# Hybrid block, attention stage: the next image's normalisation gets its rate through a PSUM bank and VectorE, nine key tiles later

## The chip, the cores and the metric

The kernel runs on one core of one Trainium2 chip. The metric is the device time of one execution in microseconds (us); less is better. The core has a matrix engine (PE), a vector engine (DVE), an activation engine (ACT), a general-purpose engine (POOL) and a queue engine (SP) that issues the DMAs. Each engine executes its own instructions in the order in which they were issued to it, and waits on semaphores for the others. PE writes to PSUM banks; ACT and DVE read and write both PSUM and SBUF; POOL here works on SBUF only.

## The reference

Input `x` is 4 images of 128 channels x 64 x 64. Layer 0 is a state-space convolution block. Layer 1 takes each image as 4096 tokens of 128 channels; its first half is the additive attention that this case is about:

```python
def _L1_attn_ref(x, Wt, Wx, bh, Wa, ba):            # x: (4, 4096, 128), 32 hidden units
    q = jnp.einsum('bld,ud->blu', x, Wt)
    k = jnp.einsum('bld,ud->blu', x, Wx)
    beta = jnp.tanh(q[:, :, None, :] + k[:, None, :, :] + bh)
    alpha = jnp.tanh(jnp.einsum('bsju,u->bsj', beta, Wa[:, 0]) + ba[0])
    alpha = jax.nn.softmax(alpha, axis=-1)
    return jnp.einsum('bsj,bjd->bsd', alpha, x)

x = x + _L0_conv_ref(_gn(x), ...)                    # layer 0
t = _to_tokens(x)
t = t + _L1_attn_ref(_ln_t(t), ...)                  # _ln_t: (v - m) / sqrt(var + 1e-5) over channels
t = t + _L1_ffn_ref(_ln_t(t), ...)                   # a recurrence over the tokens
```

## The kernel before

Three stages run one after the other: layer 0 up to about 4045 us of the span, the attention (`_rational`) to about 11340 us, and the recurrence (`_chunked`) after it. Only the attention is touched.

`_rational` writes the sum over the 32 units of tanh as a few quotients of products. Keys and queries become products of exponentials (`F` for the keys of an image, `E` and `cE` for a block of 512 queries), and a matmul over groups of 64 or 32 rows gives a denominator (`pd` bank) or a numerator (`pn` bank) for 128 keys x 512 queries.

The order of the work is written out by hand. The outer loop is over 4 images `b`, the next one over 8 blocks `s` of 512 queries (so 32 blocks in all, counted 0 to 31 here), and the inner one over 32 key tiles `jt` of 128 keys. In each key tile there are three units, A, B1 and B2, with two banks each:

- PE: `lower` makes the unit's denominators into `pd` (2 buffers of two banks), `upper` its numerators into `pn` (3 single banks); both are line L1212.
- ACT: `inverse` takes Ln of a denominator (L1231) and Exp of the negative (L1232), 1024 columns each, into an `ra` (3 buffers) or an `rb` (4 buffers) tile in SBUF.
- DVE: `times` multiplies each half with its `pn` bank (L1227).
- POOL: adds the units, `ra + rb` for B1 at L1349 and for B2 of the tile before at L1334.
- DVE: adds the two halves of the tile before into its slice of `A` (L1346). Slice `A[:, jt, :]` holds the scores of key tile `jt`.

At the end of a block ACT takes tanh and exp of all of `A` (L1384, L1385), and PE multiplies with the transposed image `xT` into the single bank named `ct` (L1360, pool `psW`, one buffer, function `pw`). The last twelve of these products, key tiles 20 to 31, are done in key tiles 2 to 13 of the next block (the dictionary `middle`).

Small steps are put between the key tiles by the dictionary `between`: what is entered at `jt` is issued at the end of that tile's work. The tuples at the head of the file say at which tile:

- `CLOSE_AT = (14, 16, 17, 18, 19, 20, 22)`: the closing of the block before: the copy from `ct`, the softmax denominator, four reciprocals (DVE, L1258), and `end` (PE L1262, DVE product L1263, POOL add `xr + rec` L1264 and the store).
- `NORM_AT = (15, 17, 19, 20)`: the four steps of `norm_steps` for 512 columns of the next image. They occur in all blocks of images 0 to 2, so in 24 blocks.
- `QUERIES_AT = (24, 26)`: the two query exponentials of the next block, which use the `ct` bank: PE L1134, ACT L1135, and a maximum on DVE (L1137).

In the first block of an image, `turn` (four PE transposes and a DVE copy) is also put in at tiles 22 to 29, and in block 0 at 16 to 23.

The four steps of `norm_steps` are `centre` (PE mean into a `pn` bank, DVE subtraction in place), `square` (ACT Square into an `rb` buffer named `sq`), `rate` (PE mean of the squares into a `pn` bank; ACT Ln at L71 and Exp of -0.5 times it at L72, in `_rsqrt`), and `scale` (POOL product in place, L1164). The normalised image is used by the next image's first queries, keys and transposes, all after the block in which the step is done, except that the last block of an image reads columns 0 to 511, normalised seven blocks before.

Of the kernel before, what the change touches and what calls it, by code (L numbers as in the profile page):

```python
# [9 lines left out]
AF = mybir.ActivationFunctionType  # L10
ALU = mybir.AluOpType
# [15 lines left out]
JT = L // P  # L27
# [13 lines left out]
PARTS = ((0, 4), (4, 12), (12, 20), (20, 32))  # L41
LAST_PARTS = ((0, 8), (8, 16), (16, 24), (24, 29), (29, 32))
CLOSE_AT = (14, 16, 17, 18, 19, 20, 22)
NORM_AT = (15, 17, 19, 20)
QUERIES_AT = (24, 26)
NOW = 20
REACH = 21.0
# [5 lines left out]
def _mm(nc, out, lhsT, rhs, n, start=True, stop=True):  # L53

    for c in range(0, n, MM):
        nc.tensor.matmul(out[:, c : c + MM], lhsT, rhs[:, c : c + MM], start=start, stop=stop)  # L56
# [12 lines left out]
def _rsqrt(nc, out, var, eps):  # L69

    nc.scalar.activation(out, var, AF.Ln, bias=eps)  # L71
    nc.scalar.activation(out, out, AF.Exp, scale=-0.5)  # L72
# [73 lines left out]
@with_exitstack  # L146
def _bounded(
    ctx: ExitStack,
    tc: tile.TileContext,
    flag,  # L150
    x1,
    x, in_wT, conv_w, conv_b, sa_w, sa_b, xpT, xpR, dtwT, dtb, A_quads, Ds,
    on_g, on_b, n1_g, n1_b, out_wT, WtT, WxT, Wt, Wx, bh, Wa, ba, W, WT, VT, gamma, beta,
    out,
):
    nc = tc.nc
    const = ctx.enter_context(tc.tile_pool(name="fconst", bufs=1))
    dram = ctx.enter_context(tc.tile_pool(name="gdram", bufs=1, space=DRAM))
    k = _Consts(tc, const)
    x2 = dram.tile([B, P, L], F32, name="x2")  # L160

    with tc.manual_schedule():
        _layer0(tc, k, x, x1, in_wT, conv_w, conv_b, sa_w, sa_b, xpT, xpR, dtwT, dtb, A_quads, Ds,
                on_g, on_b, n1_g, n1_b, out_wT)
    top = const.tile([P, TOPS], F32, name="top")
    with tc.manual_schedule():
        _rational(tc, k, x1, x2, top, Wt, Wx, bh, Wa, ba)
    with tc.manual_schedule():
        _chunked(tc, k, flag, top, x2, W, WT, VT, gamma, beta, out)
# [876 lines left out]
def _rational(ctx, tc, k, x1, x2, top, Wt, Wx, bh, Wa, ba):  # L1046
# [8 lines left out]
    nc = tc.nc  # L1055
# [14 lines left out]
    def pd():  # L1070
        return psD.tile([P, 2, QB], F32, name="pd", tag="pd")

    def pn():
        return psN.tile([P, QB], F32, name="pn", tag="pn")

    def pw():
        return psW.tile([P, QB], F32, name="ct", tag="ct")
# [23 lines left out]
    ps = pd()  # L1101
# [6 lines left out]
    ps = pd()  # L1108
# [20 lines left out]
    blocks = [slice(c * QB, (c + 1) * QB) for c in range(nq)]  # L1129
    tops = iter(range(TOPS))  # L1130

    def exponent(ps, w, src, i, out, bias=0.0):

        nc.tensor.matmul(ps, w[:, i * P : (i + 1) * P], src, start=True, stop=True)  # L1134
        nc.scalar.activation(out, ps, AF.Exp, bias=bias)  # L1135
        n = next(tops)
        nc.vector.tensor_reduce(top[:, n : n + 1], ps, AX.X, ALU.max)  # L1137


    def norm_load(b, xn, cols):  # L1140
        nc.sync.dma_start(xn[:, cols], x1[b, :, cols])

    def norm_steps(xn, cols, alloc):

        xc = xn[:, cols]
        n = cols.stop - cols.start
        held = {}

        def centre():
            ps = alloc()  # L1150
            _mm(nc, ps, k.avg, xc, n)
            nc.vector.tensor_tensor(xc, xc, ps, ALU.subtract)

        def square():
            held["sq"] = rb.tile([P, CH], F32, name="sq", tag="rb")[:, 0:n]
            nc.scalar.activation(held["sq"], xc, AF.Square)

        def rate():
            ps = alloc()
            _mm(nc, ps, k.avg, held["sq"], n)  # L1160
            _rsqrt(nc, held["sq"], ps, k.eps5)

        def scale():
            nc.gpsimd.tensor_tensor(xc, xc, held["sq"], ALU.mult)  # L1164

        return centre, square, rate, scale

    def keys(F, xn, c, ps, i):

        exponent(ps, w_k, xn[:, blocks[c]], i, F[:, i, blocks[c]], b_k[:, i : i + 1])  # L1170
# [100 lines left out]
    xn = two.tile([P, L], F32, name="xn")  # L1271
# [13 lines left out]
    A = big.tile([P, JT, QB], F32, name="A")  # L1285
    E = two.tile([P, 2, QB], F32, name="E")
    for i in range(2):
        keys(F, xn, 0, pn(), i)
# [3 lines left out]
    start = 0  # L1292
# [3 lines left out]
    for c in range(1, nq):  # L1296
        for i in range(2):
            between.setdefault(2 * c - 2 + i, []).append(lambda c=c, i=i, xn=xn: keys(F, xn, c, pw(), i))
    for c in range(nq):
        between.setdefault(16 + c, []).append(lambda c=c, xn=xn: turn(xT, xn, c))  # L1300
    for b in range(B):
        upcoming = None
        for s in range(nq):
# [4 lines left out]
            if b + 1 < B:  # L1308

                if s == 0:  # L1310
                    upcoming = two.tile([P, L], F32, name="xn")
                norm_load(b + 1, upcoming, blocks[s])
                for at, go in zip(NORM_AT, norm_steps(upcoming, blocks[s], pn)):
                    between.setdefault(at, []).append(go)
            if more:
                E_next = two.tile([P, 2, QB], F32, name="E")
# [47 lines left out]
            held = {}  # L1364
# [33 lines left out]
            if more:  # L1398
                nc.vector.tensor_tensor(A[:, 0, :], held["A"][:, 0, :], held["A"][:, 1, :], ALU.add)
                first = held["first"]  # L1400
                start = 1
# [11 lines left out]
            if turned:  # L1413
                xn = upcoming
# [250 lines left out]
```

## Time and profile before

| what | value |
|---|---|
| median of 3 runs (lowest to highest) | 11600.68 us (11594.8 to 11604.92) |
| the profiled execution: its time, its span | 11599.52 us, 11597.8 us |
| mean granted TensorE clock | 0.935 |
| attention stage, 4045 to 11340 us: PE, ACT, DVE, POOL busy | 7057, 7024, 5513, 5194 us of 7295 |
| L1164 POOL `xn<-xn,sq`, 128x512 | 24 of 1.27 us (and 4 of 128x1024 before the first block) |
| L1156 Square, L71 Ln, L72 Exp on ACT, 128x512 | 24 each, 0.61, 0.67 and 0.63 us |
| L1264 POOL `xr<-xr,rec`, 128x512 | 32 of 1.27 us |

The span runs from the first to the last instruction of the profiled execution; its time is that of the same execution, and the median comes from three executions. Where a line of the profile has a bracket, it says how long the engine was idle before the instruction and who released it. A group of instructions has its count after an x. PEclk is the granted share of TensorE's clock.

### The profile page before, as it was taken

How to read it: one execution, taken by the hardware profiler on the slowest of the kernel's cores; microseconds unless marked ns; L12 is line 12 of the kernel's file. 1: busy time of each engine (PE TensorE's matmuls, PEld its weight loads, DVE VectorE, ACT ScalarE, POOL GpSimd, SP SyncE). 2: the span in 40 equal slices, each digit the busy share in tenths (PEclk: the TensorE clock that was granted, in tenths of full speed). 3: DMA queues.
4: the chain of work that ended last, by engine and by line, in shares of the span. 5: the costliest groups of instructions: out<-in, count | busy, mean ns of one | idle time of the engine just before them, and what ended most of it. 6: DMA issues, size and time to landing. Idle time of an engine off the chain costs nothing.

```text
span 11597.8 us, 111820 instructions
## 1 busy us (share of the span) xinstructions
PE 10265.4 (89%) x36210; PEld 3139.3 (27%) x36210; DVE 8992.9 (78%) x10066; ACT 9467.7 (82%) x10209; POOL 8626.5 (74%) x3703
## 2 busy tenths in 40 slices
PE   6787787778777699999999999999999999999997
PEld 2121121122111132232233223323323233333334
DVE  4998899889889677777777777777777777777773
ACT  3556656656555599999999999999999999999995
POOL 3999889889889677767766776767677767776773
PEclk8898898888888799999999999999999999999998
DMA  4888778778778300000000000000000000000001
GB/s 118 189 182 195 169 179 192 178 173 190 180 169 194 85 1 3 6 3 4 6 3 3 3 6 3 3 3 6 3 3 3 6 2 3 3 4 3 2 3 60
DMA packets 225333, 737.77 MB, mean 64 GB/s; under 512 B 41105, under 2 KB 41937, under 8 KB 223713
## 3 DMA queue, kind: packets, MB, share of 16 engines
q1 hardware_dynamic: 221760, 729.96, 26.7%
q8 instruction: 286, 4.69, 0.2%
q14 instruction: 311, 2.54, 0.1%
q10 hardware_dynamic: 2976, 0.58, 0.0%
HBM read 612.95 MB, written 117.44 MB: 63 GB/s over the span
## 4 chain that ended last, share of the span: by engine, by line
PE 50%; ACT 10%; DVE 3%; issue 3%; POOL 0%; DMA 0%; POOLq 0%; DVEq 0%; SPq 0%; ACTq 0%
PE pn L1212 26%; PE pd L1212 16%; PE ct L1360 4%; ACT A L1384 4%; ACT A L1385 2%; DVE rb L1227 2%; ACT rb L1231 1%; ACT rb L1232 1%; PE ct L1134 1%; ACT ra L1231 1%; PE vy L1559 1%; DVE A L1346 0%; PE ct L1262 0%; PE pn L56 0%; ACT L1384 0%
## 5 line engine op out<-in xcount | busy, mean ns | idle before, releaser
L1212 PE MATMUL pn<-cE,F 32*128 32x512 f32 (+1 forms) x12288 | 4691.2, 651 | 189.9 <-DVE rb L1227 86.0
L1212 PE MATMUL pd<-E,F 32*128 32x512 f32 (+1 forms) x12288 | 3481.5, 649 | 20.4 <-DVE ra L1239 15.5
L1349 POOL TENSOR_TENSOR ra<-ra,rb 128x1024 f32<-128x1024 f32 x993 | 2637.0, 2656 | 1077.5 <-DVE rb L1227 1077.3
L1227 DVE TENSOR_TENSOR rb<-rb,pn 128x512 f32<-128x512 f32 x3972 | 2566.0, 681 | 960.0 <-ACT rb L1232 369.5
L626 POOL TENSOR_TENSOR dBu<-dtdu,bbcc 128x1024 f32<-128x1024 f32 x1024 | 2397.9, 2367 | 217.8 <-DMA dtdu<-ddd 158.8
L1334 POOL TENSOR_TENSOR ra<-ra,rb 128x1024 f32<-128x1024 f32 x993 | 2345.6, 2362 | 228.4 <-DVE rb L1227 123.9
L1232 ACT ACTIVATE rb<-rb 128x1024 f32<-128x1024 f32 x1986 | 2099.5, 1057 | 62.9
L1231 ACT ACTIVATE rb<-pd 128x1024 f32<-128x1024 f32 x1986 | 2004.6, 1009 | 112.5 <-PE pn L1212 84.9
L1212 PEld LDWEIGHTS pn<-cE,F 32*128 32x128 f32 (+1 forms) x12288 | 1367.1, 186 | 2553.9 <-DVE rb L1227 1386.2
L668 PE MATMUL py<-h,gather 128*32 128x512 f32 x4096 | 1300.7, 701 | 471.3 <-POOL h L651 359.7
L1227 DVE TENSOR_TENSOR ra<-ra,pn 128x512 f32<-128x512 f32 x1986 | 1288.2, 683 | 528.1 <-PE pn L1212 325.0
L1212 PEld LDWEIGHTS pd<-E,F 32*128 32x128 f32 (+1 forms) x12288 | 933.2, 186 | 1646.9 <-issue 820.7
L621 ACT ACTIVATE pa<-dtdu,a_neg 128x1024 f32<-128x1024 f32 x1024 | 1145.2, 1118 | 53.1 <-DVE h L641 32.1
L651 POOL TENSOR_TENSOR h<-h,bbcc 128x1024 f32<-128x1024 f32 x384 | 911.7, 2374 | 346.0 <-ACT carry L649 336.5
L641 DVE TENSOR_TENSOR_SCAN pa<-pa,carry,dBu 128x1024 f32<-128x1024 f32 x480 | 1124.5, 2343 | 23.1 <-ACT pa L621 11.3
L1232 ACT ACTIVATE ra<-ra 128x1024 f32<-128x1024 f32 x993 | 1049.7, 1057 | 31.4
L1360 PE MATMUL ct<-A,xT 128*128 128x512 f32 x2048 | 1052.3, 642 | 8.8 <-ACT A L1385 8.8
L1231 ACT ACTIVATE ra<-pd 128x1024 f32<-128x1024 f32 x993 | 1001.3, 1008 | 31.7 <-PE pd L1212 26.4
L649 ACT COPY carry<-pa 128x1 f32<-128x1 f32 x640 | 102.5, 160 | 1044.2 <-DVE h L648 1042.2
L1346 DVE TENSOR_TENSOR A<-ra 128x512 f32<-128x512 f32 x993 | 743.3, 749 | 115.9 <-POOL ra L1334 115.8
L648 DVE TENSOR_TENSOR h<-pa,bbcc 128x1024 f32<-128x1024 f32 x640 | 783.8, 1225 | 59.0 <-PE py L668 0.9
L641 DVE TENSOR_TENSOR_SCAN h<-pa,carry,dBu 128x1024 f32<-128x1024 f32 x288 | 675.0, 2344 | 171.0 <-PE py L668 141.1
(291 smaller groups left out, 8740.9 us busy)
## 6 DMA issues: line engine op xcount, KB each, us to landing
bbcc<-bcd SPq DMA_DIRECT2D x1024, 256.0 KB, 6.9
dtdu<-ddd SPq DMA_DIRECT2D x1024, 256.0 KB, 7.2
ddd<-dd SPq DMA_DIRECT2D x64, 1024.0 KB, 5.1
src<-src SPq DMA_DIRECT2D x64, 512.0 KB, 8.3
xs<-in_x_dram SPq DMA_DIRECT2D x16, 512.0 KB, 7.5
src<-xs SPq DMA_DIRECT2D x16, 512.0 KB, 3.0
bcd<-bc SPq DMA_DIRECT2D x64, 128.0 KB, 2.0
src<-xsT SPq DMA_DIRECT2D x16, 512.0 KB, 5.4
```

The lines of the kernel that those rows point to most:

```text
L621: nc.scalar.activation(dA, its[m].DT[r][:, 0, :], AF.Exp, scale=a)
L626: nc.gpsimd.tensor_tensor(dBu, its[m].DT[r][:, 1, :], its[m].BC[q][:, 0, :], ALU.mult)
L641: nc.vector.tensor_tensor_scan(to[:, step], dA[:, step], live.pop(("dBu", u))[:, step], 0.0 if m % nch == 0 else its[m - 1].carry[:, col : ...
L651: nc.gpsimd.tensor_tensor(h, h, cc, ALU.mult)
L668: nc.tensor.matmul(it.y[to, c], gather, live["h", v][:, c], start=False, stop=(q == QS - 1))
L1212: nc.tensor.matmul(ps[a], F[lo:hi, i, jt * P : (jt + 1) * P], side[lo:hi, i, :], start=True, stop=True)
L1227: nc.vector.tensor_tensor(r[:, a, :], r[:, a, :], ns[a], ALU.mult)
L1231: nc.scalar.activation(r, d, AF.Ln, scale=LOWER)
L1232: nc.scalar.activation(r, r, AF.Exp, scale=-1.0)
L1334: nc.gpsimd.tensor_tensor(rA_, rA_, rB2_, ALU.add)
L1349: nc.gpsimd.tensor_tensor(rA, rA, rB1, ALU.add)
L1360: nc.tensor.matmul(ct, xT[:, jt, :], A[:, jt, :], start=(jt == 0), stop=(jt == JT - 1))
```

## The change

The blocks of the main loop take their four norm steps from a new function, `norm_within`, and the third and fourth step are put in at key tiles 28 and 29 instead of 19 and 20. `square` writes into the slice `A[:, JT - 1, :]` (JT is 32), which is free between key tile 13 and the end of the loop, instead of an `rb` buffer. `rate` takes the `ct` bank instead of a `pn` bank, and its Exp writes its result back into that bank. `scale` is a product on DVE with the bank instead of a product on POOL with an SBUF tile. `centre` is as before. The four steps ahead of the first block still use `norm_steps`.

```diff
-NORM_AT = (15, 17, 19, 20)
+NORM_AT = (15, 17, 28, 29)
...
+    def norm_within(xn, cols, A):
+        xc = xn[:, cols]
+        held = {}
+
+        def centre():
+            ps = pn()
+            nc.tensor.matmul(ps, k.avg, xc, start=True, stop=True)
+            nc.vector.tensor_tensor(xc, xc, ps, ALU.subtract)
+
+        def square():
+            nc.scalar.activation(A[:, JT - 1, :], xc, AF.Square)
+
+        def rate():
+            held["ps"] = ps = pw()
+            nc.tensor.matmul(ps, k.avg, A[:, JT - 1, :], start=True, stop=True)
+            nc.scalar.activation(A[:, JT - 1, :], ps, AF.Ln, bias=k.eps5)
+            nc.scalar.activation(ps, A[:, JT - 1, :], AF.Exp, scale=-0.5)
+
+        def scale():
+            nc.vector.tensor_tensor(xc, xc, held["ps"], ALU.mult)
+
+        return centre, square, rate, scale
...
-                for at, go in zip(NORM_AT, norm_steps(upcoming, blocks[s], pn)):
+                for at, go in zip(NORM_AT, norm_within(upcoming, blocks[s], A)):
                     between.setdefault(at, []).append(go)
```

## The prediction

> **What bounds the kernel now.** The page comes first. In its 40 slices ACT stands at 9 from slice 15 to the last but one, so the attention stage (the L12xx and L13xx lines, 4045 to 11340 us) is the place to read, and the rest of the kernel is not touched. There I take one undisturbed stretch late in a block, and one around the norm, from the busy time by windows:
>
> ```profile
> core 0: us, PE busy (x) PEld busy (x) DVE busy (x) ACT busy (x) POOL busy (x), PEclk, DMA share, GB/s
> 5553.00:5569.00 16.00, 13.93 (x48) 3.80 (x48) 10.80 (x14) 11.12 (x12) 10.88 (x6) 0.79 0.05 17
> 10800.00:10822.00 22.00, 21.52 (x88) 6.79 (x86) 17.98 (x29) 21.65 (x23) 18.14 (x9) 1.00 0.00 1
> ```
>
> In the undisturbed 22 us ACT is busy 21.65 (98%); in the 16 us after a norm it is busy 11.12 (70%), and the granted clock is 0.79. One key tile there takes 6.0 us: three Ln (L1231) and three Exp (L1232), about 1.0 us apart, fill ACT. POOL needs 2.68 (L1349) + 2.37 (L1334) = 5.05 us per tile, 0.95 free. DVE needs seven operations of 0.68 = 4.8 us, 1.2 free. So work costs what it puts on ACT, or what it makes ACT wait for.
>
> ACT's waits are the next view (images 0 to 2, blocks 1 to 23):
>
> ```profile
> ACT rb L1231 <- PE pn L1212: 65.3, 26, 3.4
> ACT ra L1231 <- PE pd L1212: 23.3, 20, 1.9
> ```
>
> About one pair of waits per block, and in the timeline nearly all lie at key tiles 22 and 23, just after the norm's last step. The timeline of one such place, block 6 (key tiles 20 to 22):
>
> ```profile
> 5550.14 1.27 POOL L1164 TENSOR_TENSOR xn<-xn,sq 128x512 f32<-128x512 f32 x1
> 5551.38 2.36 POOL L1334 TENSOR_TENSOR ra<-ra,rb 128x1024 f32<-128x1024 f32 x1
> 5552.07 1.28 DVE L1227 TENSOR_TENSOR rb<-rb,pn 128x512 f32<-128x512 f32 x2 [0.72 <-ACT rb L1232]
> ...
> 5553.69 2.35 POOL L1349 TENSOR_TENSOR ra<-ra,rb 128x1024 f32<-128x1024 f32 x1
> 5553.77 2.82 DVE L1346 TENSOR_TENSOR A<-ra 128x512 f32<-128x512 f32 x1 [0.42 <-POOL ra L1334]
> ...
> 5557.25 1.70 PE L1212 MATMUL pn<-cE,F 64*128 64x512 f32 x2 [2.07 <-DVE rb L1227]
> ...
> 5560.90 2.08 PE L1262 MATMUL ct<-ct_s,fix 128*128 128x512 f32 x2
> 5561.06 1.02 ACT L1231 ACTIVATE rb<-pd 128x1024 f32<-128x1024 f32 x1 [3.02 <-PE pn L1212]
> ```
>
> This is the whole mechanism. The norm's scale (L1164) puts 1.27 us into POOL, which has 0.95 free, so L1334 ends late, and POOL goes straight on to L1349. Usually DVE's sum L1346 starts 0.2 us ahead of L1349 and takes 0.68; here L1349 is first by 0.08 us, and L1346 takes 2.82: it ends 0.55 us after L1349 does. DVE's products behind it are late by 2.1, PE waits 2.07 for a pn bank, its matmuls slow down (L1262 2.08 against 1.13 for the same pair elsewhere), and ACT waits 3.02, then 1.67. That L1346 has such a tail is seen in its own view:
>
> ```profile
> L1346 DVE TENSOR_TENSOR A<-ra x993: 682/683/2858, 4057.5 to 11335.4; 128x512 f32<-128x512 f32 x199
> ```
>
> Through the timeline I counted those over 1 us: 30. In all 24 blocks that have a norm there is just one, and the POOL operation two before it is L1164. The other six are in the last image, which has no norm: there the closing's add L1264, of the same 1.27 us, does it:
>
> ```profile
> 10824.42 1.28 POOL L1264 TENSOR_TENSOR xr<-xr,rec 128x512 f32<-128x512 f32 x1
> 10825.64 2.37 POOL L1334 TENSOR_TENSOR ra<-ra,rb 128x1024 f32<-128x1024 f32 x1
> ...
> 10828.00 2.35 POOL L1349 TENSOR_TENSOR ra<-ra,rb 128x1024 f32<-128x1024 f32 x1
> 10828.05 2.86 DVE L1346 TENSOR_TENSOR A<-ra 128x512 f32<-128x512 f32 x1 [0.19 <-POOL ra L1334]
> ```
>
> In the norm blocks L1264 follows two tiles after L1164, into the hole that the stall has made, and does nothing more. This decides what the change is worth.
>
> [...] L1346 (both inputs SBUF) 2.82 against 0.68, while L1227 (one input PSUM) is 625 to 690 ns in all 5958, POOL busy or not. [...] clock 0.79 around the stall, 1.00 outside, and stalls that cost 1.5 to 5 us after the same 2.1 us on DVE. [...] No attention line of this trace shows ACT writing PSUM.
>
> **The change, part by part.** The order of issue moves only these, in each of 24 blocks:
>
> - POOL loses L1164: 24 x 1.27 = 30 us of POOL, and with it the trigger at tiles 20 to 22. I summed ACT's idle pieces over 0.15 us from its timeline, block by block: block 0 5.0, blocks 1 to 23 89.5 (mean 3.89), together 94.5 us. A block's loop less this idle time is 191.7 us in norm blocks, whatever the idle, so it adds fully to the time.
> - What is late next: L1264, 1.27 > 0.95, keeps its place. The last image is the sample: blocks 25 to 31, alike in structure, idle 2.29, 1.60, 2.19, 0.39, 3.76, 3.74, 3.29, mean 2.47 (six of seven stall). Block 24, where the image's first transposes put PE and DVE work beside L1264, does not stall, 0.98. Blocks 8 and 16 are like 24; block 0 has no closing and so no L1264. Expected: 21 x 2.47 + 2 x 0.98 + 0 = 54 us. The difference, 94.5 - 54 = **40.5 us less**.
> - DVE gains the product with the bank, 24 x 0.68 (L1227, the same form: one input PSUM[...]) = 16 us, at tile 29. It stands behind the sum L1346 and ahead of two L1227, which PE (pn banks) and L1349 await. 0.68 fits in 1.2 free; the reciprocals L1258 (0.95) at tiles 17 to 20 and the maxima L1137 (0.69) at 25 and 27 stand in the same place, and no ACT wait follows them outside the stalls. Cost 0; at worst, with that cover gone, 24 x 0.68 = 16 us. In blocks 8 and 16 the copy of a transpose (0.68) is also at tile 29: 1.36 beside 1.2 free, but 1.3 of extra ACT work stands just before it, so 0 there too.
> - Rate moves from tile 19 to 28: one PE matmul pair (1.13), Ln 0.67 and Exp 0.63. All are on ACT in both places: 24 x 1.3 = 31 us there and here, difference 0. At 19 no ACT wait preceded it (its matmul ran 2 us ahead); the same holds at 28. The Exp now writes PSUM: [...] I take 0.
> - The bank: rate takes the single ct bank in place of one of three pn banks. Its last reader before, the second query's maximum, ends near tile 27, 11 us ahead of the matmul by block 6's times (Exp E of tile 26 at 5589.5, tile 28 near 5601). The next user, the weighted sum after the tanh (table load 5620.1), comes over 10 us after the product. New waits, DVE on the Exp: the Exp ends about a tile earlier. None costs.
> - Square writes the A slice 31 instead of an rb buffer: last read at tile 13, rewritten after tile 31; duration as now (0.61). An rb buffer that was held from tile 17 to 21 comes free; ACT shows no wait on it, so 0. The scaled image is next needed after the block. No DMA is moved: SP's order is the same, and POOL issues none here.
>
> Sum against the profiled execution (span 11597.8, time 11599.5): 11559.0; the median of the runs is 1.2 higher, so about **11559.5**. A measurement of this kernel can tell about 0.2%, 23 us, from no change.
>
> **The rivals.**
> 1. The closing's add takes over the stall at full size (17 in 100). If all 21 blocks cost as blocks 29 to 31 (3.6) and the PSUM product takes 5: 94.5 - 76 - 2 - 5 = 12 us less, 11588, within 0.2%. For it: six of seven stall. Against it: their size is spread 1.2 to 3.8.
> 2. No stall at all is left (7 in 100): Square at 17 shifts the phase enough that L1346 wins the race, which it loses by only 0.05 to 0.08 us. Idle 0.4 per block: 94.5 - 10 = 84 less, 11515. Against: the pattern is 6.0 us periodic again three tiles after any insert.
> 3. Slower (8 in 100): the product on DVE at tile 29 holds two L1227 back, PE runs short of pn[...], and ACT waits as at 5561. A stall of 3.9 in each of 24 blocks is 94 - 40 = 54 more, 11653; it decides from 1.7 us a block. Against: L1258, longer, does nothing of this in the same place.
>
> **How the numbers follow.** Forecast (40 less) 68, rival 1 17, rival 2 7, rival 3 8 in 100. The likeliest case spans about 20 to 65 less by the seven-block sample (all 1.6: 58 less; all 3.3: 23 less). The range reaches into rival 1 and some way to rival 2: 11522 to 11594. Faster 0.75 (forecast, rival 2), same 0.17, slower 0.08.
>
> **What would show it.** Right: no long L1346 behind a norm step in any block, about 18 behind L1264 in blocks 1 to 23, block 0 with none; ACT's waits on PE in images 0 to 2 near 50 us instead of 89; [...] ACT's busy time unchanged; no ACT wait at tiles 28 to 30. Wrong: long L1346 at 21 of 21 with mean idle above 3.3, or a new ACT wait at 29.

## The result, and the profile after

The changed kernel takes 11569.47 us (median of 9 runs, 11565.84 to 11572.52) against 11600.68 us (9 runs), 31.2 us less: the ratio is 0.9973 with a 95% interval of 0.9963 to 0.9983. The forecast was 41 us less. The profiled execution spans 11564.9 us, 32.9 less than before. The lines of the new kernel from the old L1167 on are 25 higher: L1227 is now L1252, L1346 is L1371, L1349 is L1374, L1334 is L1359, L1264 is L1289. L1189 is the new product on DVE, L1186 the Exp into the bank.

First the busy time by windows, for block 6: the 12 us in which the norm's product used to stand, and 16 us from the long sum behind the closing's add on.

```profile
core 0: us, PE busy (x) PEld busy (x) DVE busy (x) ACT busy (x) POOL busy (x), PEclk, DMA share, GB/s
5539.00:5551.00 12.00, 12.00 (x51) 3.59 (x49) 9.06 (x16) 11.75 (x13) 10.16 (x5) 1.00 0.01 1
5553.00:5569.00 16.00, 14.22 (x50) 4.10 (x50) 11.06 (x15) 11.90 (x14) 9.72 (x5) 0.79 0.10 33
```

The old place runs at full clock now, ACT busy 98%. A little later the picture of before is back: ACT 74%, clock 0.79. ACT's waits on the matmuls in images 0 to 2, from the view of waits:

```profile
ACT rb L1256 <- PE pn L1237: 45.2, 24, 3.1
ACT ra L1256 <- PE pd L1237: 16.4, 22, 1.4
```

Together 62 us, where there were 89. And the timeline of block 2 shows what makes them, tile 22 to 24:

```profile
4642.52 1.26 POOL L1289 TENSOR_TENSOR xr<-xr,rec 128x512 f32<-128x512 f32 x1
4643.75 2.36 POOL L1359 TENSOR_TENSOR ra<-ra,rb 128x1024 f32<-128x1024 f32 x1
...
4646.11 2.35 POOL L1374 TENSOR_TENSOR ra<-ra,rb 128x1024 f32<-128x1024 f32 x1
4646.14 2.87 DVE L1371 TENSOR_TENSOR A<-ra 128x512 f32<-128x512 f32 x1 [0.18 <-POOL ra L1359]
...
4649.66 2.05 PE L1237 MATMUL pn<-cE,F 64*128 64x512 f32 x2 [1.78 <-DVE rb L1252]
...
4653.66 2.08 PE L1134 MATMUL ct<-xn,w_q 128*128 128x512 f32 x2
4653.82 1.02 ACT L1256 ACTIVATE rb<-pd 128x1024 f32<-128x1024 f32 x1 [3.09 <-PE pn L1237]
```

It is the same chain as before with another first link: the closing's add in the place of the norm's product. POOL starts L1374 0.03 us ahead of DVE's sum, the sum takes 2.87 us, PE runs out of pn banks (1.78 us idle), its matmuls slow down (2.08 us for the L1134 pair here, 1.12 for the same pair of the second query, at 4667.27), ACT waits 3.09. The brackets show why POOL is first here: the sum waits for L1359, and POOL goes from L1359 straight on to L1374. In the new kernel 28 sums are over 1 us (30 before). None follows a norm step. 21 are in blocks 1 to 23, in all of them except 8 and 16; 7 are in the last image.

The operations that the change put in, from the views of their lines:

```profile
L1186 ACT ACTIVATE ct<-A x24: 601/602/602, 4230.3 to 9474.6; 128x512 f32<-128x512 f32 x24
L1189 DVE TENSOR_TENSOR xn<-xn,ct x24: 678/680/682, 4236.7 to 9481.1; 128x512 f32<-128x512 f32 x24
```

Minimum, median and maximum in ns stand after the count. Neither varies by more than 4 ns, and neither view names a wait before them or anybody who waits for them.

### The profile page after: what moved, and what is told of

Read it like the earlier page. It is cut to its first block, busy times and chain, and to the rows that moved or that the text cites. A ratio compares the mean times of both kernels' runs of the same rounds, so it can differ in the third digit from the quotient of the medians.

```text
span 11564.9 us, 111803 instructions
## 1 busy us (share of the span) xinstructions
PE 10239.8 (89%) x36210; PEld 3131.2 (27%) x36210; DVE 9001.9 (78%) x10090; ACT 9471.8 (82%) x10209; POOL 8600.2 (74%) x3679
## 4 chain that ended last, share of the span: by engine, by line
PE 49%; ACT 10%; DVE 3%; issue 3%; POOL 0%; DMA 0%; POOLq 0%; DVEq 0%; SPq 0%; ACTq 0%
PE pn L1237 25%; PE pd L1237 16%; PE ct L1385 4%; ACT A L1409 3%; ACT A L1410 2%; DVE rb L1252 2%; ACT rb L1256 1%; ACT rb L1257 1%; PE ct L1134 1%; ACT ra L1256 1%; PE vy L1584 0%; DVE A L1371 0%; ACT L1409 0%; ACT L1068 0%; PE ct L1287 0%
## 5 line engine op out<-in xcount | busy, mean ns | idle before, releaser
L1374 POOL TENSOR_TENSOR ra<-ra,rb 128x1024 f32<-128x1024 f32 x993 | 2638.4, 2657 | 1063.9 <-DVE rb L1252 1063.9
L1252 DVE TENSOR_TENSOR rb<-rb,pn 128x512 f32<-128x512 f32 x3972 | 2566.4, 681 | 959.8 <-ACT rb L1257 365.1
L1359 POOL TENSOR_TENSOR ra<-ra,rb 128x1024 f32<-128x1024 f32 x993 | 2346.5, 2363 | 243.9 <-DVE rb L1252 146.7
L1252 DVE TENSOR_TENSOR ra<-ra,pn 128x512 f32<-128x512 f32 x1986 | 1290.5, 684 | 498.7 <-PE pn L1237 314.2
L1371 DVE TENSOR_TENSOR A<-ra 128x512 f32<-128x512 f32 x993 | 740.5, 746 | 109.4 <-POOL ra L1359 109.4
```

The costliest lines, as they stand in the source:

```text
L1252: nc.vector.tensor_tensor(r[:, a, :], r[:, a, :], ns[a], ALU.mult)
L1359: nc.gpsimd.tensor_tensor(rA_, rA_, rB2_, ALU.add)
L1374: nc.gpsimd.tensor_tensor(rA, rA, rB1, ALU.add)
```

## The experiments

The theory: an extra POOL operation of 1.27 us in a plain tile makes DVE's sum start behind the next POOL add, where it takes 2.8 us and not 0.68, and all of ACT's waits inside a block come from that; which of two such operations does it is a matter of which comes first. The rivals: the late place as such is the gain; POOL's work as such is what costs; the PSUM bank plays no part. All runs are against the kernel before, on one chip per group (its median there 11598 to 11601). A sum over 1 us is called long, and ACT's idle pieces over 0.15 us inside the blocks are added up as in the prediction (before: 94.5 us in blocks 0 to 23, 18.2 in the last image; changed kernel: 64.1 and 18.1).

### e1: late, but on POOL

```diff
-            nc.scalar.activation(ps, A[:, JT - 1, :], AF.Exp, scale=-0.5)
+            nc.scalar.activation(A[:, JT - 1, :], A[:, JT - 1, :], AF.Exp, scale=-0.5)
-            nc.vector.tensor_tensor(xc, xc, held["ps"], ALU.mult)
+            nc.gpsimd.tensor_tensor(xc, xc, A[:, JT - 1, :], ALU.mult)
```

> The four norm steps stay at tiles 15, 17, 28, 29, but Exp writes the A slice and the product is again POOL's, of 1.27 us. Theory (an extra POOL operation of 1.27 us does not fit in the 0.95 us that POOL has free per tile[...]): a second long sum (2.8 us) appears after the product in each of 24 blocks, beside the closing's one, and ACT waits 1 to 4 us more per block, less where the block's end covers it: 11590 to 11650 us. Rival (only the place mattered: late in a block there is room for it): as the changed kernel, 11569 within 10 us, no long sum behind the product.

Measured: 11614.3 us, ratio 1.0013 (1.0006 to 1.0020), slower than the kernel before. 51 long sums: 24 behind the product (one in each block that has a norm), 21 behind the closing's add, 6 in the last image. ACT's waits in images 0 to 2:

```profile
ACT rb L1256 <- PE pn L1237: 90.7, 46, 3.4
```

46 waits where the changed kernel has 24. So the late place is no gain by itself, and POOL has no room there either. It is worse than before by 14 us; ACT's idle pieces grow by as much in blocks 0 to 23 (109.3 us against 94.5). At tile 20 the product's stall had hidden the closing's add two tiles later (e6 below tests that); apart from each other both are paid.

### e2: late, on DVE, but from SBUF

```diff
-            nc.scalar.activation(ps, A[:, JT - 1, :], AF.Exp, scale=-0.5)
+            nc.scalar.activation(A[:, JT - 1, :], A[:, JT - 1, :], AF.Exp, scale=-0.5)
-            nc.vector.tensor_tensor(xc, xc, held["ps"], ALU.mult)
+            nc.vector.tensor_tensor(xc, xc, A[:, JT - 1, :], ALU.mult)
```

> As the changed kernel, but Exp writes the A slice, so that the DVE product at tile 29 has two SBUF inputs and none in PSUM. Theory [...]: the product stands right behind L1346, when L1349's add has started, so it takes some 2.5 to 3 us instead of 0.68 in all 24 blocks; DVE is late by 2 us and ACT waits up to 4 us per block: 11590 to 11660 us. Rival (DVE has the time and the PSUM bank is no part of it): product 0.68 us, 11569 within 10 us.

Measured: 11633.2 us, ratio 1.0028 (1.0016 to 1.0040). The product's own line, and its place in the timeline of block 6:

```profile
L1189 DVE TENSOR_TENSOR xn<-xn,A x24: 2115/2842/2852, 4242.5 to 9540.1; 128x512 f32<-128x512 f32 x24
```

```profile
5614.40 2.67 POOL L1374 TENSOR_TENSOR ra<-ra,rb 128x1024 f32<-128x1024 f32 x1 [1.72 <-DVE rb L1252]
5614.78 2.85 DVE L1189 TENSOR_TENSOR xn<-xn,A 128x512 f32<-128x512 f32 x1
...
5618.28 2.07 PE L1237 MATMUL pn<-cE,F 64*128 64x512 f32 x2 [2.19 <-DVE rb L1252]
...
5622.46 1.02 ACT L1256 ACTIVATE rb<-pd 128x1024 f32<-128x1024 f32 x1 [3.52 <-PE pn L1237]
```

POOL's add ends at 5617.07 and the product 0.56 us after that. With the same engine, the same place and the same number of elements, a second input in SBUF instead of PSUM makes 0.68 us into 2.84 and costs 64 us in all. In the changed kernel too, all 24 products start while L1374 runs on POOL (0.37 to 1.10 us after its start), and take 0.678 to 0.682 us. This is what the PSUM bank is for.

### e3 and e4: the closing's add left out, and moved to a query's tile

e3, and then e4:

```diff
             nc.vector.tensor_tensor(held["rec"], held["rec"], num, ALU.mult)
-            nc.gpsimd.tensor_tensor(xr, xr, held["rec"], ALU.add)
             nc.sync.dma_start(x2[b, :, blocks[s]], xr)
```

```diff
-CLOSE_AT = (14, 16, 17, 18, 19, 20, 22)
+CLOSE_AT = (14, 16, 17, 18, 19, 20, 22, 26)
...
             nc.vector.tensor_tensor(held["rec"], held["rec"], num, ALU.mult)
+
+        def finish():
             nc.gpsimd.tensor_tensor(xr, xr, held["rec"], ALU.add)
             nc.sync.dma_start(x2[b, :, blocks[s]], xr)
...
-        return [take, denominators] + [lambda i=i: invert(i) for i in range(parts)] + [end]
+        return [take, denominators] + [lambda i=i: invert(i) for i in range(parts)] + [end, finish]
```

> The changed kernel with the closing's POOL add left out in all 32 blocks: the store then writes the input without the attention's part. Theory (all that is left of ACT's waits at tiles 24 and 25 comes from this add): no long sum in any block; ACT's idle pieces, 64 us in blocks 0 to 23 and 18 in the last image, fall to under 10 in all: 11569 - 70 = 11495 to 11505 us. Rival (the wait comes from the closing's PE and DVE work at tile 22, the matmul pair L1287 and the product L1288): 11555 to 11570.

> The changed kernel with the closing's last POOL add and its store moved from tile 22 to tile 26, where the second query puts 0.58 us more on ACT; PE and DVE work of the closing stay at 22. Theory (POOL has 0.95 free in a plain tile and 0.95 + 0.48 = 1.43 in a tile with a query, more than 1.27): no long sum, the same gain as leaving the add out, 11495 to 11510 us, with the result complete. Rival (any place costs the same, since POOL's free time per tile is what it is): 11560 to 11580, long sums at tile 27 or 28 instead.

Measured: e3 11478.1 us, ratio 0.9895 (0.9879 to 0.9912); e4 11485.4 us, 0.9903 (0.9886 to 0.9919). Both gained more than I had expected, 91 and 84 us against the changed kernel: the loops of e3 are 88 us shorter, where the idle pieces account for 79. e3 has no long sum at all; e4 has one, in block 31, which has no query:

```profile
L1370 DVE TENSOR_TENSOR A<-ra x993: 682/685/693, 4060.5 to 11221.3; 128x512 f32<-128x512 f32 x199
```

ACT's idle pieces are 3.6 us in e3 and 6.1 in e4, in all 32 blocks. So the add was the cause of what was left, and not the closing's matmul or product, which stayed. In e4's timeline (block 6, tiles 26 and 27) the add is there in full:

```profile
5561.81 1.27 POOL L1291 TENSOR_TENSOR xr<-xr,rec 128x512 f32<-128x512 f32 x1
5563.04 2.37 POOL L1361 TENSOR_TENSOR ra<-ra,rb 128x1024 f32<-128x1024 f32 x1
5565.44 0.69 DVE L1373 TENSOR_TENSOR A<-ra 128x512 f32<-128x512 f32 x1
5565.66 2.68 POOL L1376 TENSOR_TENSOR ra<-ra,rb 128x1024 f32<-128x1024 f32 x1 [0.26 <-DVE rb L1252]
```

POOL is idle 0.26 us before L1376, where a plain tile leaves it 0.9 to 1.0: it still waits for a DVE product, so the sum starts first, and takes 0.69. The query's Exp of 0.58 us on ACT, just before, has stretched the tile.

### e5: early, on DVE, from a pn bank

```diff
-NORM_AT = (15, 17, 28, 29)
+NORM_AT = (15, 17, 19, 20)
-            held["ps"] = ps = pw()
+            held["ps"] = ps = pn()
```

> The changed kernel with the four steps back at tiles 15, 17, 19 and 20; rate takes a pn bank as before (the ct bank is in use there), Exp writes that bank and DVE multiplies with it. So the engine and the bank change, the place does not. Theory (what counts is that POOL is spared the product): no long sum before the closing's add, which then makes one in some 21 blocks; as the changed kernel, 11569, or up to 25 us more since a pn bank is held for a tile longer: 11565 to 11595. Rival (the late place is the gain): as before, 11600 or more.

Measured: 11592.3 us, ratio 0.9994 (0.9985 to 1.0002): inside the range, though near its end, and not told apart from before. Neither side is as it was drawn. As the theory says, the product leaves no long sum at tile 20, and the closing's add makes one in the same 21 blocks (28 in all). But the profile has two things that the theory did not. Tiles 20 and 21 of blocks 0 to 23 are 14.9 us longer together than in the changed kernel (0.38 us in most blocks, 2.7 in blocks 9 and 17): PE waits 16 us there for the pn bank that the product still holds. And the same 21 long sums come out dearer by 6 us, since more of them are of the largest size (see "The size of one stall" below). The profiled execution also has a first stage that ends at 4055 instead of 4046 us, where nothing differs; whether all its runs have that can't be read from one profile, and this execution is 6 us above the median. So the gain of the changed kernel does not come from the late place alone (e1), and DVE alone, in the old place, does not show one: the late place adds a free bank, worth some 15 us in these profiles.

### e6: the kernel before without the closing's add

The edit is e3's, on the kernel before.

> The kernel before with the closing's POOL add left out in all 32 blocks (the store writes the input without the attention's part). Theory (in a norm block the product's stall at tile 20 hides the closing's add two tiles later): norm blocks keep one long sum each and their idle time of 94 us; only the last image's 18 us go, so 11600 - 18 = 11582 us, within 8. Rival (the two adds cost independently of each other): as much as the same edit did to the changed kernel, 91 us less, 11510.

Measured: 11574.9 us, ratio 0.9978 (0.9971 to 0.9985), 26 us less, where the same edit took 91 us from the changed kernel. All 24 long sums of images 0 to 2 stay, with 97.6 us of idle pieces; the last image's fall from 18.2 to 1.3. That is the masking, shown: before the change the closing's add cost nothing that can be seen in blocks 1 to 23, since the product's stall stood two tiles ahead of it.

### e7 and e10: how long may the insert be?

The changed kernel, with the add cut in two at tiles 22 and 23: 256 + 256 columns in e7 (pieces of 0.71 to 0.74 us, less than the 0.95 that the prediction left POOL in a plain tile), 448 + 64 in e10 (the first piece 1.14 us, more than that). The edit of e10; e7 has 256 in both places:

```diff
-CLOSE_AT = (14, 16, 17, 18, 19, 20, 22)
+CLOSE_AT = (14, 16, 17, 18, 19, 20, 22, 23)
...
-            nc.gpsimd.tensor_tensor(xr, xr, held["rec"], ALU.add)
+            add(0, 448)
+
+        def add(lo, hi):
+            nc.gpsimd.tensor_tensor(xr[:, lo:hi], xr[:, lo:hi], held["rec"][:, lo:hi], ALU.add)
+
+        def finish():
+            add(448, QB)
             nc.sync.dma_start(x2[b, :, blocks[s]], xr)
...
```

> The changed kernel with the closing's POOL add cut into two halves of 256 columns (about 0.65 us each), at tiles 22 and 23. Theory [...]: no long sum from it, 11480 to 11500 us. Rival (any POOL operation in between turns the race, whatever its size): 11560 to 11600, one or two long sums per block.

> The changed kernel with the closing's POOL add cut into 448 columns (about 1.13 us) at tile 22 and 64 at tile 23. How sharp is the race? L1346 lost it by 0.03 to 0.06 us in every block, so theory (the order of two starts, and nothing gradual): an insert shorter by 0.14 us loses it nowhere, 11480 to 11495, no long sums. Rival (the free time of a plain tile, 0.95 us, is the border, since 1.13 is above it): long sums in most blocks, 11555 to 11580.

Measured: e7 11481.6 us, ratio 0.9901 (0.9885 to 0.9918); e10 11479.6 us, 0.9896 (0.9879 to 0.9912). No long sum in either. The pieces of e10 in POOL's line, and its sums:

```profile
L1292 POOL TENSOR_TENSOR xr<-xr,rec x64: 307/730/1144, 4421.0 to 11264.1; 128x448 f32<-128x448 f32 x32, 128x64 f32<-128x64 f32 x32
```

```profile
L1377 DVE TENSOR_TENSOR A<-ra x993: 682/685/694, 4060.8 to 11220.5; 128x512 f32<-128x512 f32 x199
```

An insert of 1.14 us costs nothing and one of 1.27 costs about 3 us a block. The border is therefore not the 0.95 us of a plain tile that the prediction worked with, but lies between 1.14 and 1.27. The 0.95 counted the add L1349 at 2.68 us; where it starts ahead of the sum it takes 2.35 (2.345 to 2.356 in the 28 places of the changed kernel), so 0.33 of the 2.68 goes with the sum's earlier start. How near e10 comes to the border is seen in its block 6:

```profile
5537.82 1.13 POOL L1292 TENSOR_TENSOR xr<-xr,rec 128x448 f32<-128x448 f32 x1
5538.91 2.36 POOL L1365 TENSOR_TENSOR ra<-ra,rb 128x1024 f32<-128x1024 f32 x1
5541.31 0.69 DVE L1377 TENSOR_TENSOR A<-ra 128x512 f32<-128x512 f32 x1
5541.39 2.83 POOL L1380 TENSOR_TENSOR ra<-ra,rb 128x1024 f32<-128x1024 f32 x1
```

The sum starts 0.03 us after the end of the POOL add that it waits for, in the 28 long sums of the changed kernel as in the same 28 places of e10. In the changed kernel POOL's next add has started by then, 0.03 to 0.06 us earlier. In e10 POOL is idle for 0.10 to 0.13 us first, and the sum is ahead by 0.07 to 0.10. So it is a matter of which of two instructions starts first, and in these places the sum was second wherever POOL's next add had nothing left to wait for.

### e8: the product twice

```diff
+            nc.vector.tensor_tensor(A[:, JT - 1, :], xc, held["ps"], ALU.mult)
             nc.vector.tensor_tensor(xc, xc, held["ps"], ALU.mult)
```

> The changed kernel with the DVE product at tile 29 done twice, once into the free A slice, so 0.68 us more of DVE in each of 24 blocks, in the same place. My step (the product fits in the 1.2 us that DVE has free per tile, so it costs nothing): two of them, 1.36, are 0.16 over what is free, so at most 24 x 0.2 = 5 us: 11567 to 11576. The slower rival (work on DVE there makes PE short of pn banks[...]): a stall of 1.7 us or more per block, 11610 or more.

Measured: 11589.3 us, ratio to before 0.9993 (0.9986 to 1.0000); above what I expected and below the rival. Tile 30 is 0.29 us longer than in the changed kernel (6.29 against 6.00), in blocks 8 and 16 about 0.7 longer, in block 0 about 1, so the second product's own cost is about 21 x 0.29 + 2 x 0.7 + 1 = 8.5 us, as a small overflow and not as a stall. The rest of the 20 us is not beside it: 7 us are in the last image, where nothing was edited (idle pieces 25.5 against 18.1). The same stall has three sizes (see below), 17 of the 27 here are of the largest and 11 of 28 in the changed kernel, and so a total moves by some 10 us from one profile to the next. The expectation had left that out.

### e9 and e11: the kernel before, with nothing moved to another engine

e9 puts the POOL product into the tile of the first query and the closing's add into that of the second (with `finish` as in e4); e11 leaves both where they were and cuts each into halves at successive tiles. Of both edits, the tuples:

```diff
-NORM_AT = (15, 17, 19, 20)
+NORM_AT = (15, 17, 19, 24)                             # e9
+NORM_AT = (15, 17, 19, 20, 21)                         # e11
-CLOSE_AT = (14, 16, 17, 18, 19, 20, 22)
+CLOSE_AT = (14, 16, 17, 18, 19, 20, 22, 26)            # e9
+CLOSE_AT = (14, 16, 17, 18, 19, 20, 22, 23)            # e11
```

> The kernel before, so the product stays on POOL with its rb buffer, but the product goes from tile 20 to 24 and the closing's add and store from 22 to 26, the two tiles in which a query puts 0.48 us more on ACT. Theory (1.43 us free there against 1.27): no long sum in nearly any block, and with that the time of the changed kernel with the add at 26, 11480 to 11500; neither PSUM nor DVE is needed for the gain. Rival (an rb buffer held for seven tiles, or POOL's load, brings waits of its own): 11540 to 11600.

> The kernel before, nothing moved to another engine: the norm's POOL product is cut into two halves of 256 columns at tiles 20 and 21, and the closing's POOL add into two at 22 and 23. Theory (only the length of one POOL insert decides): no long sum, 11480 to 11500 us, as with the changed kernel and the add in halves. Rival (four POOL inserts in a row add up over the tiles, 2.9 us against 4 x 0.95): long sums at tile 23 or 24, 11540 to 11600.

Measured: e9 11489.0 us, ratio 0.9906 (0.9890 to 0.9923), one long sum (block 31); e11 11487.0 us, 0.9904 (0.9887 to 0.9920), none. ACT's waits in images 0 to 2 of e9:

```profile
ACT F L1178 <- PE pd L1176: 24.5, 19, 3.7
ACT rb L1231 <- PE pn L1212: 1.7, 4, 0.9
```

Of the 65.3 us that the second line had before, 1.7 are left, with the product still on POOL. What is left are the keys at an image's end. So neither PSUM nor DVE is needed for the gain: the length of one insert and its place are. This also answers the rival that POOL's work as such costs: e11 leaves POOL all of it. e4, e7, e9, e10 and e11 all beat both kernels, by 111 to 119 us against before, and their intervals overlap; no choice among them is shown.

## Why the prediction was right, and where it was not

**The mechanism and its heir.** That the product on POOL had made each norm block's long sum, and that without it the closing's add would make one, is shown: by the profile after, by e6 (the add costs nothing while the product stalls) and by e3 (nothing is left without it). e2 shows the same from the other side: a DVE product that starts 0.38 us behind L1374 takes 2.84 us with both inputs in SBUF, and 0.68 with one in PSUM. What in the hardware makes the difference is not shown by these runs.

**The term that was mis-sized.** The step "21 x 2.47 + 2 x 0.98" took its stall from seven blocks of the last image. Blocks 0, 8 and 16 came out as named, without a long sum (0, 0.67 and 1.16 us). But the others all stalled, 21 of 21 and not six of seven, with a mean of (64.1 - 0.67 - 1.16) / 21 = 2.96. That is 10 us of gain less; ACT's waits on PE came out at 62 us and not near 50. The seven blocks were a small sample of a stall with three sizes: one of them had no long sum and one the smallest stall, while of the 21 one has the smallest, eleven the middle one and nine the largest. (The prediction's last line adds 1.2 to 11559.0 and writes 11559.5; 11560.2 follows, which changes nothing here.)

**The sum by stages.** The time in the 32 loops over key tiles fell from 6246.4 to 6221.1 us, by 25.3, where the idle pieces fell by 30.4. The sentence that a loop less its idle pieces is the same "whatever the idle" missed 5 us: with the stall in tile 24 there are waits under my threshold of 0.15 us, some 0.25 a block. A further 5.6 us came from where I had looked for nothing: the stretch between an image's last tile and the next one's first fell from 50.4 to 48.6 us, three times. There PE has its slow key matmuls (1.05 to 1.22 us each, the others 0.59 to 0.70) among the first eight, in the kernel before among the next eight, and each time the granted clock is 0.50 over just these (for example 5834.14 to 5837.55 us, and before 5854.61 to 5858.02). In the other kernels the same stretch takes mostly one or the other (e4: 50.25, 48.55, 48.60) with no relation to the edits, so I do not put it down to the change; why the half rate falls on the first or on the next eight is not shown. The last 2.0 us lie behind the loops, almost all in the recurrence, which was not edited. 25.3 + 5.6 + 2.0 = 32.9. The forecast of 40.5, without the 10 us of larger stalls and the 5 below the threshold, would have been 25; that 32.9 came out is in part luck, 7.6 us that were not forecast and are not shown to be the change's.

**The steps at no cost.** The product on DVE: 0.680 us, no ACT wait behind it in plain blocks (tile 30 is 6.00 us there); in blocks 8 and 16, which I had put at 0, tile 30 is 0.3 us longer. The Exp into PSUM: 0.602 us, against 0.630 into SBUF before and, at the same place, in e1; 0.7 us in all, where the prediction took 0. The Ln, the Square and the single ct bank: no wait.

**The rivals.** Rival 1, the stall taken over at full size, is the nearest: 21 of 21, but a mean of 2.96 and not 3.6. Rival 2, no stall left, is what e4 and e7 get with one more edit: its 84 us less were too small by 30 to 35, since it left the last image's stalls, and the waits under 0.15 us, where they were. The way it named, that Square at tile 17 lets the sum win, did not happen. Rival 3 asked whether DVE work at tile 29 starves PE: e8 doubles it and finds 0.29 us in a plain block; only e2, where the product takes 2.84 us, brings that stall.

**The size of one stall.** One lost race costs ACT 1.2 us in one block and 4 in the next, though PE's gap behind the long sum is 1.77 or 1.78 us in all 28 places of the changed kernel. What differs is the granted clock. It is either full or half in these records (1.00 or 0.50), and within the attention stage all its changes, 117 in the changed kernel and 121 in the one before, lie within 0.02 us of one grid of 3.413 us in each trace. The next lines show 10.24 us, three steps of that grid, from its first point after the start of PE's gap, in blocks 1, 3 and 2 of the changed kernel:

```profile
4424.44:4434.68 10.24, 9.71 (x40) 3.13 (x40) 8.21 (x14) 8.91 (x10) 7.39 (x3) 1.00 0.00 0
4878.41:4888.65 10.24, 10.24 (x42) 3.19 (x46) 7.00 (x11) 7.77 (x9) 6.93 (x3) 0.83 0.00 0
4649.72:4659.96 10.24, 10.24 (x28) 2.84 (x28) 6.01 (x10) 6.25 (x7) 5.22 (x3) 0.67 0.01 2
```

The granted clock, third from the end, is 1.00, 0.83 and 0.67: no step, one step and two steps at half rate. ACT's idle time in these stalls is 1.21, 2.42 and 3.93 us. Over all 28 there is no overlap: 3 stalls without half rate cost 1.21 us each, 14 with one step 2.19 to 2.45, 11 with two 3.11 to 3.94; the groups of e8 fit these. Which it is goes with the place on the grid at which PE starts again after the gap: a start 0.5 to 1.1 us after a point has none, 1.4 to 2.5 us one, and from 0.7 us ahead of a point to 0.3 after it two. A gap of 1.78 us, about half a step, was followed by half rate in 25 of the 28 places.

**What stays open.** This relation is read from the traces, and was not tested by shifting a gap on purpose. What sets a kernel's place on the grid is not known, so neither is how to choose the cheap size. Why e5's first stage is 9 us longer is open too.

## What to carry to other kernels

Before an operation is moved off a crowded engine, look for the next operation of the same length on that engine: a stall that is removed may only have been standing in front of another one, and its gain is the difference of the two. Where a POOL and a DVE operation hold each other up, as the add L1374 (2.35 us or 2.68) and the sum L1371 (0.68 or 2.87) do here, ask which instruction starts first, and what each of the two still waits for, not only how much time is free: cutting an insert in two, or placing it in a tile that another engine has just stretched, may be worth more than moving it. And if a DVE operation must run beside POOL, try it with one input in PSUM: here that made 0.68 us of 2.84 (e2).

## What the runs showed of the hardware that I had not expected

- How steep the border is: a POOL insert of 1.144 us costs nothing, one of 1.27 about 3 us a block; 0.13 us less in that one place, with the rest of the add a tile later, is worth about 90 us of the kernel (11569 against 11480).
- How much one lost race grows: 2.1 us late on DVE become up to 4 us of idle ACT, since PE's matmul pairs go from 1.13 to 2.08 us while the granted clock is at half. After the gaps of 1.77 or 1.78 us that was for none, one or two steps of 3.41 us, and the stall had three sizes accordingly (1.21, 2.19 to 2.45, 3.11 to 3.94 us).
- That the profiles of programs alike but for a small edit differ by some 7 to 10 us in stalls that the edit did not touch (25.5 against 18.1 us in the last image of e8). There is one profile of each program, so how much of this changes from one execution to the next is not known; the 20 runs of e8 span 9.7 us.
